# Layer 0 of a four-layer graph network: expert weights ordered behind adj's last rows, degree work ordered behind the expert blocks' outputs, and the last group's gate put in front of the blocks

## The chip, the cores and the metric

The kernel runs on one core of a Trainium2 chip. The core has TensorE (PE, matmuls, with its weight loads shown apart as PEld), VectorE (DVE), ScalarE (ACT), GpSimd (POOL) and SyncE (SP), which here only issues transfers. Each engine takes its instructions in the order in which the program holds them; semaphores tie the engines together. The metric is the device time of one execution in microseconds (us), lower is better.

## The reference, cut to what matters

There are N = 2708 nodes with 256 features each, a 2708 x 2708 matrix `adj`, and four layers, each a graph step followed by a feed-forward step. All numbers are float32. Only layer 0, and the row sums that layer 1 needs, are touched here:

```
x = x + weights(adj) @ (layernorm(x) @ W + B)         # weights = exp(-(1/r - 1)^2 / 0.5) where r < 1, else 0
h = layernorm(x)
top2 of (h @ Wg + bg) over 8 experts, softmax of the two
x = x + sum over the two of w * (gelu(h @ W1[e] + b1[e]) @ W2[e] + b2[e])
# layer 1, graph step
D = 1 / sqrt(sum of a row of (adj + I));  x = x + relu((D adj+I D) @ (layernorm(x) @ W) + b)
```

An expert has 256 x 1024 and 1024 x 256 weights. Layers 1 to 3 follow with other graph and feed-forward steps and are the same before and after.

## The kernel before, in words

The 2708 nodes are 22 tiles (`NT`) of 128 rows, the last with 20. The kernel is written against a tile framework: the Python code states the instructions, a scheduler chooses each engine's order by its own estimates, and semaphores are put in from the data dependences. `tc.add_manual_dep(..., NoSync, ...)` adds an order that the scheduler has to keep and no semaphore by itself. A pool's tile name with `bufs=n` has n buffers in turn; when a pool is closed its memory serves later pools, and what is first written there waits for the last use before.

**Adjacency of layer 0.** The target nodes are taken in three groups of 9, 7 and 6 tiles (`GROUPS`). For each group the loop over `j` (L712 and on) loads one row tile of `adjT` (`adrow`, L715, five buffers), ScalarE and VectorE turn it into weights (`weigh`, L699 to L704: Ln, Exp, a product, Exp, a mask), and PE multiplies it with `msg` into accumulators `acc` (L726). At the end of a group VectorE adds `acc` to `x` (L748).

**Gate of layer 0.** `send(tiles)` (L640 and on) runs after each group: layer norm statistics (`stats`), the normalised rows `xr` (L182 by `norm_to`), a turn by PE and a copy by ScalarE (`turn_to`, L195 and L196), the product with the 8 gate columns (L656) and the bias (`lg`, L658). Then come the two best experts (`top2_weights`), the place of each row in its expert's list (`route`, with matmuls at L344 and L346), and GpSimd's indirect scatters of the rows into `taken` in DRAM (L451). `xr` has one buffer, so the next group's `xr` waits until those scatters are done. After the second group, `blocks` makes the list of nine full blocks of 256 rows (`full`), and after the third the list of the rest (`rest`).

**Expert blocks of layer 0.** A block is 256 rows of one expert. `Blocks.run` (L523 and on) goes through 24 blocks (9 full, 15 of the rest). `fetch` (L490) reads the block's expert number into SyncE registers and issues the weight transfers `wa` (L620, W1 and its bias) and `wb` (L622, W2 and its bias), three sets of buffers in turn; `fetch_rows` gathers the rows `xs` (L465). PE turns the rows (`turn`, L518) and VectorE copies them into `xTs` (L520). PE multiplies with W1 (L547), ScalarE applies Gelu into `hTs` (L549), PE multiplies with W2 into `yacc` (L556), VectorE adds the bias and the gate's weight into `ys` (L558, L559), and GpSimd scatters `ys` into `given` (L451). The weights of blocks 0 and 1 and their rows are fetched inside the adjacency loop of the third group, at `j == NT - 5`.

**Degrees for layer 1.** Beside the blocks, `beside(b)` reads adj once more in 42 half rows of 677 KB (`adhalf`, L780, three buffers) and VectorE adds them up in `cs` (first copy L782, additions L784). It is called ahead of block b's matmuls, for row tile `j = b - 1`. After the blocks 22 small matmuls (L791) turn `cs` into the degrees.

Of the kernel before, what the change touches and what calls it, by code (L numbers as in the profile page):

```python
# [8 lines left out]
F32 = mybir.dt.float32  # L9
# [3 lines left out]
ALU = mybir.AluOpType  # L13
AX = mybir.AxisListType

P = 128
N = 2708
D = 256
# [18 lines left out]
def rows(t):  # L37
    return min(P, N - t * P)
# [28 lines left out]
def adj_ffn4(ctx: ExitStack, tc: tile.TileContext, a: dict, out: bass.AP):  # L67
# [122 lines left out]

    def turn_to(xT, xn, r):

        p = ps_tmp()
        for c in range(DC):
            te.transpose(p[:, c * P : c * P + r], xn[:, c * P : (c + 1) * P], ident[:r, :r])  # L195
        s.copy(xT, p[:, : DC * P].rearrange("p (c t) -> p c t", c=DC)[:, :, :r])  # L196
# [278 lines left out]
    class Blocks:  # L475
# [36 lines left out]

        def turn(self, pool, xs):
            xT = pool.tile([P, DC, 2 * P], F32, name="xTs", bufs=2)
            p = pools["psum"].tile([P, W], F32, name="turned", bufs=1)
            for k in range(2):
                for c in range(DC):
                    te.transpose(p[:, (c * 2 + k) * P : (c * 2 + k + 1) * P],  # L518
                                 xs[:, k, c * P : (c + 1) * P], ident)
            v.tensor_copy(xT.rearrange("p c t -> p (c t)"), p)  # L520
            return xT

        def run(self, pool, items, during=None):  # L523

# [88 lines left out]
    with ExitStack() as l0:  # L613
        hw = l0.enter_context(tc.tile_pool(name="h0", side="right", reuse_waits="tile", bufs=1))

        def weights0(b, es):

            pool, bufs = (hw, 2) if b % 3 < 2 else (hcs[0], 1)
            wa = pool.tile([P, 2048 + 8], F32, name="wa", bufs=bufs)
            nc.sync.dma_start(wa, a["L0_ffn_W1b"][bass.ds(es[0], 1)].rearrange("e p n -> p (e n)"))  # L620
            wb = pool.tile([P, 2048 + D], F32, name="wb", bufs=bufs)
            nc.sync.dma_start(wb, a["L0_ffn_W2p"][bass.ds(es[0], 1)].rearrange("e p n -> p (e n)"))  # L622
# [3 lines left out]
        hcs = []  # L626
        gate, gnn, sums = ExitStack(), ExitStack(), ExitStack()
# [12 lines left out]
        def send(tiles):  # L640

            G = len(tiles)
            t0 = tiles[0]
            st = stats(tiles)
            xr = tp.tile([P, GMAX, 2, XW], F32, name="xr", bufs=1)[:, :G]
            lg = tp.tile([P, G, E], F32, name="lg", tag=f"lg{G}", bufs=1)
            v.memset(lg[:, G - 1, :], 0.0)
            for i, t in enumerate(tiles):
                r = rows(t)
                norm_to(xr[:r, i, 0, :D], t, i, st)  # L650
                g.tensor_copy(xr[:r, i, 1, :D], xr[:r, i, 0, :D])
                xT = tp.tile([P, DC, P], F32, name="xT", bufs=2)
                turn_to(xT[:, :, :r], xr[:r, i, 0, :D], r)
                p = ps_tmp()
                for c in range(DC):
                    te.matmul(p[:r, :E], lhsT=xT[:, c, :r], rhs=wg[:, c, :],  # L656
                              start=(c == 0), stop=(c == DC - 1))
                v.tensor_tensor(lg[:r, i, :], p[:r, :E], bg[:r], ALU.add)  # L658
# [47 lines left out]
        for tiles in GROUPS:  # L706
# [5 lines left out]
            for j in range(NT):  # L712
                r = rows(j)
                ad = gp.tile([P, GMAX * P], F32, name="adrow", bufs=5)[:r, :w]
                nc.sync.dma_start(ad, a["adjT"][j * P : j * P + r, c0 : c0 + w])  # L715
                if tiles is GROUPS[0] and j % 2 == 0:
# [49 lines left out]
        cs = hp.tile([P, N], F32, name="cs")  # L766
        left = []

        def beside(b):

            j = b - 1
            if b == NA + 3:
                left.append(blocks_left(rest[2], MOST))
            if not 0 <= j < NT:
                return
            r = rows(j)
            for c0 in (0, N // 2):
                w = N // 2
                ad = hp.tile([P, N // 2], F32, name="adhalf", bufs=3)[:r]
                nc.sync.dma_start(ad, a["adjT"][j * P : j * P + r, c0 : c0 + w])  # L780
                if j == 0:
                    v.tensor_copy(cs[:, c0 : c0 + w], ad)  # L782
                else:
                    v.tensor_tensor(cs[:r, c0 : c0 + w], cs[:r, c0 : c0 + w], ad, ALU.add)  # L784

        work0.run(hc, items, beside)
        work0.run_rest(hc, more, left[0], ALWAYS)
# [760 lines left out]
```

The softmax here doesn't subtract the row's maximum and nothing guards it: scores larger than these inputs give would overflow.

## Time and profile before

| what | value |
|---|---|
| device time, median of 3 | 2094.61 us (2092.79 to 2096.02) |
| span of the profiled execution | 2097.1 us |
| PE busy | 1980.9 us, 94% of the span |
| DVE, ACT, POOL busy | 1100.6, 660.6, 288.1 us |
| mean granted clock of PE | 0.965 of full speed |
| read and written in DRAM | 206.46 MB, 20.65 MB |

In the trace the adjacency of layer 0 runs until about 272.7 us, the 24 blocks from there until 652.7 us, and layer 1 begins at about 664 us. All matmuls with 256 columns take two passes, so one matmul of the code is two in the trace: a block has 32 + 32 of them and 4 transposes.

How to read the lines shown below. A line of the timeline has the start in us from the span's start, the duration in us, the engine (SPq is SyncE's queue of transfers, for which the duration is that of issuing), the line of the code, the operation, the tile written and the tiles read, and how many instructions are merged. In brackets is the engine's idle time just before, and what ended it. A line of a table of windows has the window, its length, the busy time and count of PE, PEld, DVE, ACT and POOL, the clock granted to PE as a share of full speed, the busy share of the 16 DMA engines, and GB/s.

### The profile page before, as it was taken

The page shows a single profiled execution, that of the slowest core. Times are in us where ns is not written, and L with a number is a line of the kernel's source. Part 1 is how long each engine was busy: PE and PEld are TensorE (multiplying, and loading weights), DVE is VectorE, ACT ScalarE, POOL GpSimd, SP SyncE. Part 2 cuts the span into 40 slices and gives each one's busy share as a digit, 9 for nine tenths or more (in the row PEclk, how much of TensorE's full clock was granted, in tenths as well). Part 3 has the DMA queues.
Part 4 walks back from the last instruction along what each step waited for, and adds up shares of the span by engine and source line. Part 5 has one row for each costly group of instructions (what it writes and reads, how often), then busy time and mean ns, then how long its engine had stood idle before and what let it go on. Part 6 is the DMA issues. An engine that isn't in the chain of part 4 may idle for free.

```text
span 2097.1 us, 25890 instructions
## 1 busy us (share of the span) xinstructions
PE 1980.9 (94%) x9673; PEld 1424.7 (68%) x9673; DVE 1100.6 (52%) x2524; ACT 660.6 (31%) x1445; POOL 288.1 (14%) x315
## 2 busy tenths in 40 slices
PE   6999978999997999999899969999899999999997
PEld 5888767878885788878688848888566622232334
DVE  7677754544114323243331165455355488887876
ACT  7778732222222403022322351223243410120112
POOL 1004353333221000102142110000000000000000
PEclk9999989999997999999999989999899999999999
DMA  8435649987532442423265420000101000000000
GB/s 261 141 106 150 213 158 353 352 298 262 186 145 92 123 142 61 141 62 111 92 213 184 162 91 6 1 1 1 41 1 31 16 1 21 21 26 11 16 11 24
DMA packets 80611, 226.64 MB, mean 108 GB/s; under 512 B 15218, under 2 KB 38746, under 8 KB 71264
## 3 DMA queue, kind: packets, MB, share of 16 engines
q1 hardware_dynamic: 69056, 196.17, 28.4%
q0 software_dynamic: 11424, 28.74, 3.9%
q8 instruction: 80, 1.31, 0.3%
q14 instruction: 51, 0.42, 0.1%
HBM read 206.46 MB, written 20.65 MB: 108 GB/s over the span
## 4 chain that ended last, share of the span: by engine, by line
PE 57%; DMA 5%; issue 3%; DVE 2%; ACT 1%; POOL 1%; POOLq 0%; SPq 0%; DVEq 0%; ACTq 0%
PE num L1460 11%; PE ps_acc L1136 10%; PE acc L942 9%; PE ps_tmp L317 7%; PE den L1471 6%; DMA given<-ys,xs 4%; PE ps_acc L1312 3%; PE ps_tmp L238 3%; PE ps_acc L547 1%; PE ps_tmp L195 1%; PE ps_acc L238 1%; PE yacc L556 1%; PE ps_tmp L874 1%; DMA mine<-given 0%; POOL given L451 0%
## 5 line engine op out<-in xcount | busy, mean ns | idle before, releaser
L1455 DVE SCALAR_TENSOR_TENSOR e<-arena,G,mask 128x1024 f32<-128x1024 f32 (+2 forms) x264 | 294.1, 1149 | 44.0 <-PE den L1471 43.6
L556 PE MATMUL yacc<-wb,hTs 128*128 128x256 f32 x1152 | 267.5, 385 | 11.2 <-DVE ys L558 10.7
L556 PEld LDWEIGHTS yacc<-wb,hTs 128*128 128x128 f32 x1152 | 218.0, 193 | 44.0 <-DVE ys L558 14.6
L1460 PE MATMUL num<-e,wh 128*64 128x512 f32 (+4 forms) x1056 | 243.6, 558 | 0.0
L726 PE MATMUL acc<-msg,wt 128*128 128x256 f32 (+1 forms) x924 | 210.7, 386 | 7.9 <-DVE wt L704 7.9
L942 PE MATMUL acc<-sup,adrow 128*128 128x256 f32 (+1 forms) x924 | 214.4, 390 | 0.0
L1136 PE MATMUL ps_acc<-hh,e 128*128 128x257 f32 (+1 forms) x924 | 211.2, 386 | 0.0
L726 PEld LDWEIGHTS acc<-msg,wt 128*128 128x128 f32 (+1 forms) x924 | 175.7, 193 | 35.9 <-DVE wt L704 8.3
L942 PEld LDWEIGHTS acc<-sup,adrow 128*128 128x128 f32 (+1 forms) x924 | 176.6, 195 | 30.6 <-issue 5.5
L1136 PEld LDWEIGHTS ps_acc<-hh,e 128*128 128x128 f32 (+1 forms) x924 | 173.8, 193 | 29.6 <-issue 2.5
L547 PE MATMUL ps_acc<-xTs,wa 128*128 128x256 f32 x768 | 179.6, 385 | 8.7 <-DVE xTs L520 8.6
L1460 PEld LDWEIGHTS num<-e,wh 128*64 128x64 f32 (+1 forms) x1056 | 74.3, 138 | 155.2 <-issue 120.8
L549 ACT ACTIVATE hTs<-ps_acc,wa 128x256 f32<-128x256 f32 x192 | 89.9, 473 | 271.5 <-PE yacc L556 194.4
L547 PEld LDWEIGHTS ps_acc<-xTs,wa 128*128 128x128 f32 x768 | 142.1, 192 | 36.4 <-DVE xTs L520 11.4
L196 ACT COPY xT<-ps_tmp 128x256 f32<-128x256 f32 x126 | 43.0, 362 | 325.1 <-PE ps_tmp L195 324.0
L1471 PE MATMUL den<-e,wh 128*32 128x512 f32 (+4 forms) x1056 | 137.9, 551 | 0.0
L1133 DVE SCALAR_TENSOR_TENSOR e<-Rb,G,mask 128x640 f32<-128x640 f32 (+2 forms) x110 | 85.2, 775 | 97.1 <-PE ps_acc L1136 96.9
L451 POOL DMA_INDIRECT taken<-xr,r_ix x66 | 76.8, 1163 | 357.9 <-DVE b_vec L387 190.7
L451 POOL DMA_INDIRECT given<-ys,xs x72 | 81.8, 1136 | 229.9 <-DVE ys L559 166.0
L465 POOL DMA_INDIRECT xs<-taken,b_ix x72 | 87.2, 1212 | 189.0 <-DVE xTs L520 87.2
L919 DVE TENSOR_SCALAR mask<-adrow 128x1024 uint8<-128x1024 f32 (+1 forms) x66 | 41.6, 631 | 134.5 <-DMA adrow<-in_adjT 132.6
L558 DVE TENSOR_TENSOR ys<-yacc,wb 128x256 f32<-128x256 f32 x72 | 30.3, 421 | 155.2 <-PE yacc L556 155.0
(388 smaller groups left out, 2459.7 us busy)
## 6 DMA issues: line engine op xcount, KB each, us to landing
adhalf<-in_adjT SPq DMA_DIRECT2D x42, 677.0 KB
wb<-in_L_ffn_W2p SPq DMA_DIRECT2D x24, 1152.0 KB
wb<-in_L_ffn_Wdp SPq DMA_DIRECT2D x24, 1152.0 KB
wa<-in_L_ffn_W1b SPq DMA_DIRECT2D x24, 1028.0 KB
adrow<-in_adjT SPq DMA_DIRECT2D x42, 512.0 KB
adrow<-in_adjT SPq DMA_DIRECT2D x42, 320.0 KB
adrow<-in_adjT SPq DMA_DIRECT2D x21, 576.0 KB
adrow<-in_adjT SPq DMA_DIRECT2D x21, 448.0 KB
```

The costliest lines, as they stand in the source:

```text
L317: te.matmul(p[:, :w], lhsT=w1[:, c, f * P : (f + 1) * P], rhs=xnT[:, c, c0 : c0 + w], start=(c == 0), stop=(c == DC - 1))
L451: i = g.indirect_dma_start(out=dst, out_offset=bass.IndirectOffsetOnAxis(ap=ix, axis=0), in_=src, in_offset=None, bounds_check=bound, oob_ ...
L465: i = g.indirect_dma_start(out=dst, out_offset=None, in_=src, in_offset=bass.IndirectOffsetOnAxis(ap=ix, axis=0), bounds_check=bound, oob_ ...
L547: te.matmul(p[:, f % 2, :], lhsT=w1[:, c, f * P : (f + 1) * P], rhs=xT[:, c, :], start=(c == 0), stop=(c == DC - 1))
L549: s.activation(hT[:, f, :], p[:, f % 2, :], AF.Gelu, bias=bias[:, f : f + 1])
L556: te.matmul(q[:, k, :], lhsT=hT[:, f, k * P : (k + 1) * P], rhs=w2[k][:, f, :], start=(f == 0), stop=(f == HC - 1))
L726: te.matmul(p[:q, n - pair[0], :], lhsT=wt[:, k : k + q], rhs=msg[:r, j, :], start=(j == 0 and n == pair[0]), stop=(j == NT - 1 and n == p ...
L942: te.matmul(p[:q, n - pair[0], :], lhsT=ad[:, k : k + q], rhs=sup[:r, j, :], start=(j == 0 and n == pair[0]), stop=(j == NT - 1 and n == p ...
L1136: te.matmul(p[:q, : D + 1], lhsT=e[:r, k : k + q], rhs=hh[:r, j, :], start=(j == 0), stop=(j == NT - 1))
L1455: v.scalar_tensor_tensor(e[:r, :w], Rb[:r, k, :w], G[:r, j, 2 * pair + k, :], mask[:r, j, c0 : c0 + w], op0=ALU.max, op1=ALU.mult)
L1460: te.matmul(num[k * DK : (k + 1) * DK, hf, :q], lhsT=wh[:r, j, 2 * pair + k, :DK], rhs=e[:r, h0 - c0 : h0 - c0 + q], start=(j == 0), stop= ...
L1471: te.matmul(den[z : z + Q, :q], lhsT=wh[:ri, i, 2 * pair + k, DK : DK + 1].to_broadcast([ri, Q]), rhs=e[:ri, h0 - c0 : h0 - c0 + q], start ...
```

## The change: three orders in layer 0

1. **Expert weights behind adj's last rows.** `reads` collects adj's row loads, and each `wa` load is ordered behind the latest of them. The call of `work0.fetch` moves out of the loop over `j`, behind it, while `fetch_rows` stays. So the weight transfers no longer stand ahead of the rows that PE still needs.
2. **The last group's gate in front of the blocks.** The first turn of block 0's rows is ordered after the gate matmul of the last group's fourth tile (`gated[-3]`: the list has one entry for each tile of 22, and the third from its end is tile 19). The last group's statistics are split into the first two tiles and the other four, with the inverse root by Ln and Exp on ScalarE (`by_log`) instead of by twelve small VectorE operations, and its turns use the three `ps_acc` banks, which are free by then, instead of the two of `ps_tmp`.
3. **Degree reads and additions behind the blocks' outputs.** `beside` no longer reads from block 1 on. It starts at block 3, with three halves for each of blocks 3 to 8 and two for each of blocks 9 to 20, and adds a half one call after its read. Both the reads and the additions are ordered behind the latest scatter of a block's output (`given0`), so that VectorE does not stand at an addition while `ys` and `xTs` are behind it.

The amount of data and of arithmetic is the same but for these few operations.

```diff
-    def turn_to(xT, xn, r):
+    def turn_to(xT, xn, r, bank=None):
-        p = ps_tmp()
+        p = ps_tmp() if bank is None else bank
...
-        def turn(self, pool, xs):
+        def turn(self, pool, xs, after=None):
...
-                    te.transpose(p[:, (c * 2 + k) * P : (c * 2 + k + 1) * P],
-                                 xs[:, k, c * P : (c + 1) * P], ident)
+                    i = te.transpose(p[:, (c * 2 + k) * P : (c * 2 + k + 1) * P],
+                                     xs[:, k, c * P : (c + 1) * P], ident)
+                    if after is not None:
+                        tc.add_manual_dep(i.ins, after, mybir.DependencyInfo(
+                            mybir.DependencyClass.NoSync, mybir.DependencyReason.DATA),
+                            reason="order")
...
-            turned = self.turn(pool, self.rows[0])
+            turned = self.turn(pool, self.rows[0], after)
...
-            nc.sync.dma_start(wa, a["L0_ffn_W1b"][bass.ds(es[0], 1)].rearrange("e p n -> p (e n)"))
+            i = nc.sync.dma_start(wa, a["L0_ffn_W1b"][bass.ds(es[0], 1)].rearrange("e p n -> p (e n)"))
+            tc.add_manual_dep(i.ins, reads[-1], mybir.DependencyInfo(
+                mybir.DependencyClass.NoSync, mybir.DependencyReason.DATA), reason="order")
...
-            st = stats(tiles)
+            parts = [tiles]
+            if tiles is GROUPS[-1]:
+                parts = [tiles[:2], tiles[2:]]
+            st = {t: (z, t - part[0]) for part in parts
+                  for z in [stats(part, by_log=len(parts) > 1)] for t in part}
...
-                turn_to(xT[:, :, :r], xr[:r, i, 0, :D], r)
+                turn_to(xT[:, :, :r], xr[:r, i, 0, :D], r, ps_acc() if len(parts) > 1 else None)
...
+                gated.append(made.ins.name)
...
-                nc.sync.dma_start(ad, a["adjT"][j * P : j * P + r, c0 : c0 + w])
+                i = nc.sync.dma_start(ad, a["adjT"][j * P : j * P + r, c0 : c0 + w])
+                reads.append(i.ins.name)
...
                     for item in items[:2]:
-                        work0.fetch(item)
                         work0.fetch_rows(item)
+            for item in items[:2] if end else ():
+                work0.fetch(item)
...
+        halves = [(j, c0) for j in range(NT) for c0 in (0, N // 2)]
+        def behind_outputs(i):
+            tc.add_manual_dep(i.ins, scattered["given0"][-1].name, mybir.DependencyInfo(
+                mybir.DependencyClass.NoSync, mybir.DependencyReason.DATA), reason="order")
         def beside(b):
-            j = b - 1
...
-            if not 0 <= j < NT:
+            while read:
+                j, c0, ad = read.pop(0)
+                r, sums = rows(j), cs[:, c0 : c0 + N // 2]
+                behind_outputs(v.tensor_copy(sums, ad) if j == 0 else
+                               v.tensor_tensor(sums[:r], sums[:r], ad[:r], ALU.add))
+            if b < 3:
                 return
-            r = rows(j)
-            for c0 in (0, N // 2):
...
-        work0.run(hc, items, beside)
+            while halves and len(read) < (3 if b < NA else 2):
+                j, c0 = halves.pop(0)
+                ad = hp.tile([P, N // 2], F32, name="adhalf", bufs=3)
+                behind_outputs(nc.sync.dma_start(
+                    ad[: rows(j)], a["adjT"][j * P : j * P + rows(j), c0 : c0 + N // 2]))
+                read.append((j, c0, ad))
+        work0.run(hc, items, beside, gated[-3])
+        assert not halves and not read
```

More of the change, by code (lines that the diff above doesn't have):

```diff
@@ L517, in turn, with run @@
                 for c in range(DC):
-                    te.transpose(p[:, (c * 2 + k) * P : (c * 2 + k + 1) * P],
-                                 xs[:, k, c * P : (c + 1) * P], ident)
+                    i = te.transpose(p[:, (c * 2 + k) * P : (c * 2 + k + 1) * P],
[4 more added lines that the diff above has]
+                            reason="order")
             v.tensor_copy(xT.rearrange("p c t -> p (c t)"), p)
             return xT
-        def run(self, pool, items, during=None):
+        def run(self, pool, items, during=None, after=None):
             HC = 1024 // P
@@ L624, in weights0 @@
             return wa[:, :2048].rearrange("p (c h) -> p c h", c=DC), wa[:, 2048:], (w2, w2)
-        hcs = []
+        hcs, reads, gated = [], [], []
         gate, gnn, sums = ExitStack(), ExitStack(), ExitStack()
@@ L649, in send @@
                 r = rows(t)
-                norm_to(xr[:r, i, 0, :D], t, i, st)
+                norm_to(xr[:r, i, 0, :D], t, st[t][1], st[t][0])
                 g.tensor_copy(xr[:r, i, 1, :D], xr[:r, i, 0, :D])
                 xT = tp.tile([P, DC, P], F32, name="xT", bufs=2)
-                turn_to(xT[:, :, :r], xr[:r, i, 0, :D], r)
+                turn_to(xT[:, :, :r], xr[:r, i, 0, :D], r, ps_acc() if len(parts) > 1 else None)
                 p = ps_tmp()
                 for c in range(DC):
-                    te.matmul(p[:r, :E], lhsT=xT[:, c, :r], rhs=wg[:, c, :],
-                              start=(c == 0), stop=(c == DC - 1))
+                    made = te.matmul(p[:r, :E], lhsT=xT[:, c, :r], rhs=wg[:, c, :],
+                                   start=(c == 0), stop=(c == DC - 1))
+                gated.append(made.ins.name)
                 v.tensor_tensor(lg[:r, i, :], p[:r, :E], bg[:r], ALU.add)
@@ L766, in adj_ffn4 @@
         cs = hp.tile([P, N], F32, name="cs")
-        left = []
+        left, read = [], []
+        halves = [(j, c0) for j in range(NT) for c0 in (0, N // 2)]
+        def behind_outputs(i):
+            tc.add_manual_dep(i.ins, scattered["given0"][-1].name, mybir.DependencyInfo(
+                mybir.DependencyClass.NoSync, mybir.DependencyReason.DATA), reason="order")
         def beside(b):
-            j = b - 1
             if b == NA + 3:
                 left.append(blocks_left(rest[2], MOST))
-            if not 0 <= j < NT:
-                return
-            r = rows(j)
-            for c0 in (0, N // 2):
[L778 to L784, printed above, removed]
-        work0.run(hc, items, beside)
+            while read:
[4 more added lines that the diff above has]
+            if b < 3:
+                return
+            while halves and len(read) < (3 if b < NA else 2):
[6 more added lines that the diff above has]
+        assert not halves and not read
         work0.run_rest(hc, more, left[0], ALWAYS)
```

## The prediction

> **What bounds the kernel now.** I read the page's busy line first (PE 94% of the span), so a gain can only be PE idle time or PE time at a low clock. The edits lie in layer 0 alone: both instruction orders agree from layer 1 on. So I took a table of windows over 200 to 740 us, looked for stretches where PE is not busy, and opened the timeline there. The queue of transfers comes first:
>
> ```profile
> 243.72 0.35 SPq L620 DMA_DIRECT2D wa<-in_L_ffn_W1b  x1
> 244.25 0.34 SPq L622 DMA_DIRECT2D wb<-in_L_ffn_W2p  x1
> 245.10 0.33 SPq L620 DMA_DIRECT2D wa<-in_L_ffn_W1b  x1
> 245.62 0.65 SPq L622 DMA_DIRECT2D wb<-in_L_ffn_W2p  x1
> 246.37 1.06 SPq L715 DMA_DIRECT2D adrow<-in_adjT  x2
> ```
>
> Two experts' weights (2 x 2180 KB) go out before the last two rows of adj. The timeline shows who pays:
>
> ```profile
> 261.53 0.83 ACT L141 ACTIVATE y<-adrow,tiny 128x640 f32<-128x640 f32 x1 [9.73 <-DMA adrow<-in_adjT]
> 266.25 6.46 PE L726 MATMUL acc<-msg,wt 128*128 128x256 f32 x20 [7.91 <-DVE wt L704]
> 266.28 0.20 POOL L660 COPY xr<-choice 128x12 int32<-128x12 int32 x1 [3.85 <-DMA taken<-xr,r_ix]
> ...
> 318.76 0.87 DVE L782 COPY cs<-adhalf 128x1354 f32<-128x1354 f32 x1 [12.82 <-DMA adhalf<-in_adjT]
> ...
> 320.02 5.82 PE L556 MATMUL yacc<-wb,hTs 128*128 128x256 f32 x16 [8.67 <-DVE ys L558]
> ```
>
> PE stands 7.91 us for adj's last rows, and 8.67 us because VectorE, which works in order, stands 12.82 us at the first degree copy with the output ys behind it. The POOL line matters later: xr is only free at 266.28, when the scatters of the middle group have landed. A third stall of the second kind:
>
> ```profile
> 425.22 0.49 DVE L507 MEMSET xs<- 128x516 f32 x1 [8.31 <-DMA given<-ys,xs]
> ...
> 427.78 2.08 PE L547 MATMUL ps_acc<-xTs,wa 128*128 128x256 f32 x4 [3.24 <-DVE xTs L520]
> ```
>
> The windows give the clock after it, and the two regimes of the blocks:
>
> ```profile
> 427.50:430.00 2.50, 2.22 (x5) 1.85 (x6) 2.30 (x4) 0.00 (x0) 2.19 (x2) 0.50 0.77 228
> ...
> 340.00:425.00 85.00, 82.78 (x389) 69.69 (x387) 42.45 (x50) 22.33 (x48) 31.23 (x21) 1.00 0.94 354
> ...
> 515.00:620.00 105.00, 105.00 (x504) 90.74 (x503) 18.91 (x42) 27.80 (x59) 26.54 (x26) 1.00 0.51 181
> ```
>
> While adj is read again for the degrees (340 to 425), DMA is 94% busy at 354 GB/s; once the reads are over, PE never idles. There a block takes 14.27 us (weights issued at 531.37 and 545.64). That is the floor: 64 matmuls at 0.2155 us (83.8 us of warm PE time over 389 of them, 340 to 425) and four transposes.
>
> **What the Trainium skill says.** "TensorE: Matmul & The Clock Gate", What's actually happening: an idle window of about 3.4 us halves PE's clock, and about 3.4 us of sustained work restores it. The trace agrees: 0.50 after the 3.24 us gap, and 16 matmuls in 5.82 us after the 8.67 us one, 3.62 us elsewhere. So removing a long stall also returns 2 to 3 us of slow matmuls. "DMA: Bandwidth & Descriptors", Issuing engines are not separate DMA queues: transfers of SyncE and GpSimd interleave on the same 16 engines. The trace agrees: given scatters hold the memset for 8.31 us while adhalf and weights stream.
>
> **The change, part by part.**
>
> *Weights behind adj's last rows.* In the new order both rows precede the four weight transfers. The rows (370 KB) then need about 1 us at 354 GB/s and can't be what ScalarE waits for at 251.8. From there its chain for two rows, 5.6 us measured from 261.53 to the last wt at 267.15, ends near 257.5, before PE is through its earlier rows (258.34). So PE goes straight on: 20 matmuls x 0.22 = 4.4, end at 262.7 instead of 272.7. The weights go out about 3 us later and land (4.46 MB at 390 GB/s, the rate of 255 to 265) near 260, still ahead of use.
>
> *Gate in front.* The ten us can't all reach the blocks. The gate's first norm writes xr, so it waits for the POOL copy: 266.5. The rest of its start fits: sums and two tiles' statistics 2.8 us from 262.7, then Ln and Exp on 128x2. The trace has no such activation; the nearest, 128x6, takes 0.21, a floor is the 0.17 of small VectorE operations; I take 0.21 each. They replace twelve small VectorE operations (2.4 us). Six tiles at 1.48 us (spacing of the lg additions at 282.32 and 283.80, with blocks' matmuls between), somewhat faster here from three banks: 6 us, then the copy xTs, 0.7. The first expert matmul starts near 274, now 276.13. The gathers of its rows are issued at 267.07 and 268.46 as now and are in by 272.65 at the latest. Taking the turn after the third-last tile's gate costs nothing more.
>
> What follows on PE: 12 matmuls cold, 0.39 each as now (12 in 4.72): 278.7. The route's 14 matmuls, 1.9: 280.6. Then the second xTs copy stands behind 14 small VectorE operations (3.4 us) and takes 0.7; PE waits for it: 285. After that nothing is missing: 46 matmuls of block 0, 64 of block 1, 4 of block 2, 24.6 us, two turns within: 310. The same point is now at 325.68, after 8.67 us of stall, the cold stretch behind it, and the gate between blocks. **Gain 15.7.** ScalarE's three table loads (1.28 each, same number) fall into the waits. GpSimd's 12 scatters now stand ahead of both outputs of block 0; ys has two buffers and block 2 rewrites the first at about 318, long after 301 (12 x 1.27 from 286), so that wait is covered.
>
> *Degree reads and additions.* 42 reads of 677 KB stay, three a block from block 3, two from block 9, each added a block later behind the outputs. Now from 325.68 to the last yacc at 652.7 is 327.0 us; 22 blocks at the floor less the four matmuls, plus a microsecond of degree matmuls, is 314.1. The excess is 12.9, of which 6.3 is the one interval with the stall at 425 (421.19 to 441.79). After: three additions (3 x 1.52) start when ys is out and end about 6 us into a block, when VectorE has nothing else due; xTs is wanted at 14. A block with three reads moves 2.23 MB weights, 2.08 reads, 0.53 gathers and scatters: 4.84 MB, 13.7 us at 354 GB/s, under 14.27 but barely; with two, 4.15 MB, 11.7. The memset behind the given scatter stays on VectorE ahead of xTs, so some waits stay: I keep 4 us between bounds 0 and 12.9. **Gain 8.9.**
>
> The added waits order engines only; queued behind them are ys and xTs, which the floor of 515 to 620 shows have slack. The reads end with block 20 and the additions with 21 of 23, so the degree matmuls don't move. Memsets and the split of the stats go beside PE work.
>
> Sum 24.6: 2094.6 - 24.6 = 2070.
>
> **The rivals.**
> *Smaller gain.* The start stays bound by gathers, cold clock and the route, DMA near 95% still holds VectorE: 8 at the start, 2 later, 2085. For it: the 13.7 of 14.27 us, and xr free only at 266.28. Against: the saturated stretch shrinks from some 13 blocks to 6.
> *Everything goes.* Degree excess zero (12.9), VectorE's wait after the route filled (3) and the blocks two us earlier: 33.6, so 2061. For it: 515 to 620 without a gap. Against: the xr release.
> *Slower.* VectorE's small operations and table loads are exposed with PE cold, leaving 2 of the 15.7; and reads wait for additions, additions for reads without overlap: 4.6 + 5.9 + 6.3 (2.23 MB weights) = 16.8 a block, 15 us over six blocks, 4 won in the others: 2104. For it: three buffers, three reads. Against: each addition frees its own buffer at once.
> *Nothing.* The two losses cancel: 2094.
>
> **How the numbers follow.** Forecast 0.64 (2062 to 2079), smaller gain 0.18, everything 0.09, nothing 0.03, slower 0.06. Leaving out slower, nothing, and the outer parts of the two gain cases gives 2060 to 2085. Faster 0.91, same 0.03, slower 0.06.
>
> **What would show it.** Right: no ACT wait for adrow near 252, the adjacency's last matmul near 263; first expert matmul at 273 to 275; a PE gap of 2 to 5 us around the route; no gap near 310; last yacc near 628 (652.7 - 24.6). Wrong: an expert matmul waiting for wa or wb, a start after 278, or VectorE waiting for adhalf with ys or xTs behind it in blocks 4 to 9, seen as PE gaps and clock 0.5.

## The result and the profile after

The changed kernel takes 2078.04 us (median of 4 runs, 2076.05 to 2081.6), the kernel before 2093.73 in the same comparison: ratio 0.9925, 95% interval 0.9908 to 0.9943, so 15.7 us less. The forecast was 2070, range 2060 to 2085. A second measurement of the unchanged code of the changed kernel, made later among the experiments, gave 2069.75; why the two differ is half of what follows.

Spans differ by some us from one execution to the next before layer 0's adjacency is over, so times are best compared from a common instruction. I take **A**, the start of PE's last uninterrupted stretch of adjacency matmuls, just behind the small matmul of L261: 238.65 before, 237.29 after. The first lines to look at are of the timeline of the changed kernel:

```profile
237.29 24.20 PE L739 MATMUL acc<-msg,wt 128*128 128x256 f32 x110
...
247.21 0.83 ACT L141 ACTIVATE y<-adrow,tiny 128x640 f32<-128x640 f32 x1 [0.36 <-DMA adrow<-in_adjT]
...
260.24 0.69 DVE L762 TENSOR_TENSOR x<-x,acc 128x512 f32<-128x512 f32 x1 [4.95 <-PE acc L739]
...
267.50 0.21 POOL L672 COPY xr<-choice 128x12 int32<-128x12 int32 x1 [5.94 <-DMA taken<-xr,r_ix]
267.60 0.41 DVE L182 TENSOR_SCALAR xr<-x,mv,var 128x256 f32<-128x256 f32 x1 [3.32 <-DMA taken<-xr,r_ix]
...
268.07 1.12 PE L195 MATMUL ps_acc<-ident,xr 128*128 128x128 f32 x4 [6.57 <-DVE xr L182]
...
279.10 4.33 PE L551 MATMUL ps_acc<-xTs,wa 128*128 128x256 f32 x12 [2.12 <-DVE lg L670]
```

ScalarE's wait for adj's row has shrunk from 9.73 us to 0.36, and PE goes through 110 adjacency matmuls without a gap. The sum into x starts at A + 22.95, before at A + 32.81. Then everything waits for one thing: at 267.50 the scatters of the middle group have landed, GpSimd and VectorE may write xr again, and PE, idle for 6.57 us, begins the gate. The gate needs 11 us, so the first expert matmul is at 279.10.

One thing that now lies beside these scatters shows in the queue of transfers of the changed kernel:

```profile
261.52 0.33 SPq L629 DMA_DIRECT2D wb<-in_L_ffn_W2p  x1
```

This is block 2's W2, 1152 KB. It goes out as the last matmul of the adjacency ends, in the kernel before at 272.75, 6.5 us after the copy at 266.28 that shows xr free. The adjacency now ends some 10 us earlier, and this transfer goes out while the last of the scatters is being issued (260.58 to 261.56).

The second place is block 1. PE and then ScalarE in the timeline of the changed kernel (a releaser "issue" is idle time for which the profile shows no cause, "remote" one that it can't place):

```profile
298.42 4.50 PE L551 MATMUL ps_acc<-xTs,wa 128*128 128x256 f32 x20
306.98 4.21 PE L551 MATMUL ps_acc<-xTs,wa 128*128 128x256 f32 x8 [4.06 <-issue]
310.98 4.54 PE L560 MATMUL yacc<-wb,hTs 128*128 128x256 f32 x16
```

```profile
302.93 0.47 ACT L553 ACTIVATE hTs<-ps_acc,wa 128x256 f32<-128x256 f32 x1 [2.09 <-PE ps_acc L551]
306.45 0.47 ACT L553 ACTIVATE hTs<-ps_acc,wa 128x256 f32<-128x256 f32 x1 [3.04 <-issue]
308.59 0.97 ACT L553 ACTIVATE hTs<-ps_acc,wa 128x256 f32<-128x256 f32 x2 [1.67 <-remote]
```

Both engines stand still in the middle of a block whose weights and rows are there, and the 8 matmuls that follow take 4.21 us where four take 1.03 warm. PE goes on at 306.98, just as the Gelu of 306.45 ends (306.92), so its part looks like a wait for ScalarE to empty an accumulator; what holds ScalarE, the profile doesn't say. I call this **the stop**.

Third, the blocks with the degree reads, in a table of windows of the changed kernel (columns as before):

```profile
340.00:425.00 85.00, 85.00 (x406) 73.33 (x405) 39.98 (x52) 22.26 (x47) 30.53 (x24) 1.00 0.87 337
427.50:430.00 2.50, 2.50 (x13) 2.21 (x12) 1.24 (x3) 0.00 (x0) 0.84 (x1) 1.00 1.04 428
515.00:620.00 105.00, 104.97 (x499) 89.94 (x498) 39.59 (x57) 26.51 (x56) 32.87 (x25) 1.00 0.59 222
```

PE is busy in every one of the 85 us in which 82.78 were busy before, at full clock, with DMA at 0.87 instead of 0.94. The degree work itself now looks like this in the timeline of VectorE:

```profile
349.15 1.64 DVE L797 COPY cs<-adhalf 128x1354 f32<-128x1354 f32 x2
350.70 1.56 DVE L798 TENSOR_TENSOR cs<-cs,adhalf 128x1354 f32<-128x1354 f32 x1
```

No wait stands in brackets: the halves have been there since the block before. The memset of xs still waits for scatters of given (42.2 us in total, 51.8 before), but at most 4.9 us at a time (8.3 before), which the slack of the block covers. Another 20.0 us ahead of it, at most 5.2 at a time, have no releaser in the profile. From block 1's last matmul to the last yacc it is 315.3 us, against 327.0 before and a floor of 314.1.

### The profile page after: what moved, and what is told of

Its sections match the earlier page's. It is cut to its first block, busy times and chain, and to the rows that moved or that the text cites. A ratio compares the mean times of both kernels' runs of the same rounds, so it can differ in the third digit from the quotient of the medians.

```text
span 2075.3 us, 25886 instructions
## 1 busy us (share of the span) xinstructions
PE 1974.2 (95%) x9673; PEld 1422.3 (69%) x9673; DVE 1098.1 (53%) x2513; ACT 661.8 (32%) x1449; POOL 287.4 (14%) x315
## 3 DMA queue, kind: packets, MB, share of 16 engines
q8 instruction: 80, 1.31, 0.3%
## 4 chain that ended last, share of the span: by engine, by line
PE 55%; DMA 5%; issue 3%; DVE 2%; ACT 2%; POOL 1%; POOLq 0%; DVEq 0%; SPq 0%; ACTq 0%
PE num L1483 11%; PE acc L965 9%; PE ps_acc L1159 9%; PE ps_tmp L317 7%; PE den L1494 6%; DMA given<-ys,xs 4%; PE ps_acc L1335 3%; PE ps_tmp L238 3%; PE ps_tmp L195 1%; PE ps_acc L238 1%; PE ps_tmp L897 1%; POOL xs L465 1%; PE ps_acc L551 1%; POOL given L451 0%; DMA mine<-given 0%
## 5 line engine op out<-in xcount | busy, mean ns | idle before, releaser
L560 PE MATMUL yacc<-wb,hTs 128*128 128x256 f32 x1152 | 263.1, 381 | 0.9 <-DVE ys L562 0.7
L451 POOL DMA_INDIRECT given<-ys,xs x72 | 91.8, 1275 | 208.7 <-DVE ys L563 161.2
L942 DVE TENSOR_SCALAR mask<-adrow 128x1024 uint8<-128x1024 f32 (+1 forms) x66 | 41.5, 629 | 134.4 <-DMA adrow<-in_adjT 134.2
L465 POOL DMA_INDIRECT xs<-taken,b_ix x72 | 75.0, 1042 | 191.0 <-DVE xTs L524 90.6
```

Source lines behind the costliest of these rows:

```text
L451: i = g.indirect_dma_start(out=dst, out_offset=bass.IndirectOffsetOnAxis(ap=ix, axis=0), in_=src, in_offset=None, bounds_check=bound, oob_ ...
L465: i = g.indirect_dma_start(out=dst, out_offset=None, in_=src, in_offset=bass.IndirectOffsetOnAxis(ap=ix, axis=0), bounds_check=bound, oob_ ...
L560: te.matmul(q[:, k, :], lhsT=hT[:, f, k * P : (k + 1) * P], rhs=w2[k][:, f, :], start=(f == 0), stop=(f == HC - 1))
```

## The experiments

Three sets, each on one chip and each set on a different one, with runs of the kernel before among them (medians 2093.51, 2095.1 and 2093.81). In the table "block 1 done" is the point that the prediction called blocks 0 and 1 done and four matmuls of block 2; times are us from A in each kernel's profiled run. The forecast row is the prediction's own points, less before's A.

| kernel | first expert matmul | block 1 done | end of last yacc | median, us | ratio to before |
|---|---|---|---|---|---|
| before | 37.5 | 87.0 | 414.0 | 2093.73 | |
| forecast | 35.4 | 71.4 | 389.4 | 2070 | |
| changed | 41.8 | 82.4 | 397.7 | 2078.04 | 0.9925 [0.9908, 0.9943] |
| *first set* | | | | | |
| part 1 undone | 47.4 | 88.6 | 404.5 | 2084.63 | 0.9947 [0.9927, 0.9967] |
| part 2 undone | 36.5 | 84.1 | 399.5 | 2080.29 | 0.9934 [0.9917, 0.9952] |
| part 3 undone | 41.2 | 87.5 | 412.9 | 2087.29 | 0.9975 [0.996, 0.999] |
| twenty copies | 41.5 | 80.5 | 395.7 | 2075.51 | 0.9911 [0.9894, 0.9927] |
| *second set* | | | | | |
| own tile for the last rows | 37.4 | 72.7 | 388.2 | 2070.54 | 0.9871 [0.9849, 0.9892] |
| scatters late | 40.2 | 73.4 | 388.1 | 2072.53 | 0.9886 [0.9866, 0.9907] |
| W2 of block 3 late | 40.0 | 74.0 | 389.6 | 2072.15 | 0.9881 [0.9861, 0.9902] |
| own tile, scatters late | 37.3 | 72.5 | 388.6 | 2071.17 | 0.988 [0.9855, 0.9905] |
| *third set* | | | | | |
| changed, again | 40.0 | 74.4 | 390.1 | 2069.75 | 0.9893 [0.9878, 0.9908] |
| two more reads | 40.2 | 74.6 | 390.0 | 2071.37 | 0.9892 [0.9878, 0.9906] |
| own tile, W2 late | 37.4 | 72.5 | 387.7 | 2067.68 | 0.9885 [0.9869, 0.99] |
| own tile, gate between | 36.2 | 74.1 | 389.8 | 2071.93 | 0.989 [0.9871, 0.991] |

Behind the last yacc the code is the same in all of them, and the profiled runs spend between 1431 and 1444 us there. So a difference of a few us between medians says little about layer 0 by itself; the times from A say more, but each is from one run.

### Part 1 undone

```diff
                     for item in items[:2]:
+                        work0.fetch(item)
                         work0.fetch_rows(item)
-            for item in items[:2] if end else ():
-                work0.fetch(item)
```

(and the order of `wa` behind `reads[-1]` taken out).

> The changed kernel with its first part undone: the weights of blocks 0 and 1 are issued ahead of adj's last two rows again. If those rows set the end of the adjacency and with it the start of the gate, PE idles some 8 us at the last rows again, the last adjacency matmul ends near 272 instead of 260, and the gate's first norm moves from 267.6 to about 275: 8 to 10 us more, 2086 to 2088. If the start is held by the scatters and gathers whatever the adjacency does, PE idles but nothing behind it moves: 2078 to 2080.

The waits of the adjacency are back, in the timeline of this kernel:

```profile
264.95 0.83 ACT L141 ACTIVATE y<-adrow,tiny 128x640 f32<-128x640 f32 x1 [9.44 <-DMA adrow<-in_adjT]
...
269.67 6.39 PE L736 MATMUL acc<-msg,wt 128*128 128x256 f32 x20 [7.62 <-DVE wt L713]
```

The sum into x starts at A + 32.44 again, and the end of the last yacc is 6.8 us later than the changed kernel's by the profile, 6.6 by the medians (the intervals of the two ratios just overlap). It is less than the 9.5 us that the adjacency loses, and a second time says why: GpSimd's copy that shows xr free comes at A + 27.7 here and at A + 27.6 in the kernel before, but at A + 30.2 in the changed one. So part 1 itself pushes the release of xr back by 2.5 us. Two things that it does can account for this: the weights of blocks 0 and 1 go out later, and block 2's W2 goes out with the earlier end of the adjacency (here at 276.09, 6.0 us after that copy). At the 415 GB/s that the engines move then, the 1152 KB of W2 take 2.8 us (an estimate). No run separates the two. (In the kernels with an added tile W2 goes out at A + 19.7, and the copy still comes at A + 29.7 to 30.0; there too it lies beside the scatters.)

### Part 2 undone

```diff
-            if tiles is GROUPS[-1]:
-                parts = [tiles[:2], tiles[2:]]
...
-        work0.run(hc, items, beside, gated[-3])
+        work0.run(hc, items, beside)
```

> The changed kernel with its second part undone: the last group's gate is free to go between the matmuls of the first blocks, its statistics are in one piece and by VectorE. If the gate in front earns its place, the blocks lose again what the gate takes between them (7 to 8 us of PE time and the route's waits): 2083 to 2087. If standing in front costs as much as it brings (in the changed kernel PE is at half clock and mostly idle from 265 to 279, first expert matmul 279.1, three us later than before the change), the first expert matmul moves to 272 to 274 and the time is 2072 to 2079.

The expert matmuls begin 5.4 us earlier (A + 36.5), as soon as the gathered rows are in, in PE's timeline:

```profile
273.01 0.69 PE L518 MATMUL turned<-ident,xs 128*128 128x128 f32 x2 [9.48 <-DMA xs<-taken,b_ix]
...
275.79 5.24 PE L551 MATMUL ps_acc<-xTs,wa 128*128 128x256 f32 x12 [0.78 <-DVE xTs L524]
```

The gate then stands between the matmuls of block 0, and the lead is gone when 68 expert matmuls are done: A + 61.4 here, A + 61.1 in the changed kernel. The further lag, 1.7 us by the end of block 1, comes in the stop, which holds VectorE too here: `yacc` is complete at 311.85, but its sum into ys starts at 317.72 (9.27 us idle, releaser "remote"), and PE waits for it:

```profile
318.20 5.38 PE L560 MATMUL yacc<-wb,hTs 128*128 128x256 f32 x16 [5.49 <-DVE ys L562]
```

The medians differ by 2.3 us and the intervals overlap: the gate in front costs about what it brings.

### Part 3 undone

`beside` as in the kernel before (one row tile a block from block 1, nothing ordered behind the outputs).

> The changed kernel with its third part undone: degree reads and additions from block 1 on, as before. If the trace's account holds (12.9 us of excess over the block floor before, 1.2 after), it loses 11.7 us at least, and the 8.7 us stall at the first degree copy with its cold clock may return on top: 2089 to 2099, with clock 0.5 after a PE gap. If the third part is worth only the 4 to 9 us that the prediction gave it: 2082 to 2087.

Windows of this kernel, to be held against 85.00 of 85.00 above:

```profile
335.00:380.00 45.00, 43.96 (x209) 37.43 (x207) 22.29 (x25) 11.26 (x24) 16.42 (x12) 1.00 0.94 358
380.00:425.00 45.00, 43.16 (x196) 36.46 (x197) 24.20 (x29) 11.12 (x24) 19.19 (x12) 0.96 0.91 337
425.00:520.00 95.00, 91.14 (x423) 77.30 (x423) 41.72 (x56) 22.36 (x48) 36.82 (x26) 0.98 0.75 279
```

PE loses 6.7 us in these three windows alone, and block 1's end to the last yacc takes 325.4 us, nearly before's 327.0. By the medians part 3 is worth 9.3 us, the largest of the three. By the profile it is 15.2 (412.9 against 397.7), but the profiled run, 2092.67, is among the slowest of 13 (2084.13 to 2093.96). The three losses (6.6, 2.3 and 9.3, each against the changed kernel of the first pair, which was not in this set) add up to 18.2, a little more than the 15.7 of the whole, which at this spread is no contradiction.

### Twenty copies: is the stop tied to a place in ScalarE's program?

```diff
+            for n in range(20 if end else 0):
+                pad = small.tile([P, 1], F32, name="pad")
+                i = s.copy(pad, ones)      # ordered behind the last weights' Exp
             send(tiles)
```

> The changed kernel with 20 one-column ScalarE copies put behind the last adjacency weights, where ScalarE waits some 8 us for the sums. In both traces ScalarE stops at its 269th instruction or so, counted in the program's order (before at 305.5 for 3.8 us, after from 300.8 to 306.5), with nothing in the trace that it waits for, just behind a packet of the instruction queue (304 and 298). If it is ScalarE's instruction supply, the stop moves 20 instructions earlier in the work, off block 1: no PE gap of 4 us near 303, no half clock behind it, about 7 us less, 2070 to 2073. If it waits for data of block 1 or for crowded transfers, the stop stays at the same Gelu of block 1 and the time at 2077 to 2081.

The stop is still in block 1, 20 instructions further on in ScalarE's program, spread over more Gelus. PE's timeline of this kernel:

```profile
308.42 1.13 PE L552 MATMUL ps_acc<-xTs,wa 128*128 128x256 f32 x4 [1.75 <-ACT hTs L554]
310.56 2.07 PE L552 MATMUL ps_acc<-xTs,wa 128*128 128x256 f32 x4 [1.01 <-issue]
```

That speaks against a fixed place in ScalarE's stream. It is shorter, and the time 2.5 us lower than the changed kernel's, which no theory had asked for.

### Own tile for the last group's rows

```diff
-                norm_to(xr[:r, i, 0, :D], t, st[t][1], st[t][0])
-                g.tensor_copy(xr[:r, i, 1, :D], xr[:r, i, 0, :D])
+                xn = xr[:r, i, 0, :D] if own is None else own[:r, i, :]
+                norm_to(xn, t, st[t][1], st[t][0])
+                if own is not None:
+                    g.tensor_copy(xr[:r, i, 0, :D], xn)
+                g.tensor_copy(xr[:r, i, 1, :D], xn)
```

> The last group's normalised rows go into a tile of their own (xn_end); two GpSimd copies a tile bring them into xr, so VectorE and PE no longer wait for the middle group's scatters to leave xr. If it is the release of xr that starts the gate late, its first turn comes near 264.5 instead of 268.1; the gate still takes some 11.5 us with PE cold, so the first expert matmul comes near 275.5 instead of 279.1, and the time falls by 3 to 4 us. If block 0's rows (in at about 272.5), the cold clock or the table loads set the start of the blocks, the first expert matmul stays after 278 and the time falls by less than 1.5 us. The stop in block 1 (306.98 in the changed kernel) is expected in both cases, and if it is tied to a fixed moment of the transfers rather than to block 1, the start's gain is lost there again.

In this kernel's timeline PE's wait ahead of the gate falls to 3.14 us, and the gate is under way when GpSimd's copy comes, at 270.31, A + 29.7, about where it comes in the other kernels (the profile names PE as what released it here):

```profile
267.92 1.12 PE L195 MATMUL ps_acc<-ident,xn_end 128*128 128x128 f32 x4 [3.14 <-DVE xn_end L182]
...
270.31 0.20 POOL L678 COPY xr<-choice 128x12 int32<-128x12 int32 x1 [5.77 <-PE ps_tmp L673]
```

From A the gate starts 3.0 us earlier than in the repeated changed kernel (27.3 against 30.3), the first expert matmul is 2.7 earlier, and block 1 ends 1.6 earlier: the release of xr did hold the gate. The rest of the gain goes at the second xTs copy behind the route, for which PE waits 1.31 us here and 0.39 there. In the time it can't be told from nothing (2070.54 against 2069.75, in different sets).

### Scatters late, and W2 of block 3 late

```diff
-                for k in range(2):
-                    scatter(taken[0], ix[:r, i, k : k + 1], xr[:r, i, k, :], 2 * N - 1, "taken0")
...
+            if b == 2:
+                later.pop()()              # the same 12 scatters, ordered behind given0's latest
+                past.extend(scattered["taken0"])
+                gate.close()
```

```diff
-            nc.sync.dma_start(wb, a["L0_ffn_W2p"][bass.ds(es[0], 1)].rearrange("e p n -> p (e n)"))
+            i = nc.sync.dma_start(wb, a["L0_ffn_W2p"][bass.ds(es[0], 1)].rearrange("e p n -> p (e n)"))
+            if b == 3:
+                behind(i, scattered["given0"][1:2])
```

> The twelve scatters of the last group's rows are issued behind block 1's outputs instead of ahead of block 0's; every engine but GpSimd keeps its order, and nothing needs these rows before the gathers for block 9. If the stop of ACT and PE in block 1 (4.06 us, and some 7.7 us with the cold matmuls after it) comes from those scatters and block 3's W2 sharing the transfer engines, it leaves block 1: no gap over 1 us there, the twenty-second W1 and W2 stretch warm, point 'four matmuls of block 2' at about 312 instead of 319.7, and the time falls by 5 to 8 us unless a stop of the same kind comes where the scatters now are (316 to 332), which would give it back. If the stop has nothing to do with the scatters (a supply of instructions at a fixed place, or the W2 transfer alone), it stays at 303 to 309 and the time stays within 1.5 us.

> The W2 transfer of block 3 (1152 KB, issued at 299.07) waits until block 0's second output has landed (about 308); no instruction moves. If the stop in block 1 needs this transfer beside the twelve scatters, it goes or shrinks to under 1.5 us, and the time falls by 4 to 7 us. If the scatters alone make it, or neither does, it stays and the time is the same within 1.5 us.

> Both edits together: own tile for the last group's normalised rows and the scatters behind block 1's outputs. If both waits are what holds the start, the gains add: first expert matmul near 275.5, no stop in block 1, blocks 0 and 1 and four matmuls of block 2 done near 308 to 310 (the forecast's 310), 9 to 12 us faster than the changed kernel, about 2067. If the start is bound elsewhere, no more than the better of the two edits alone.

The stop is in none of the three: block 1 is done at A + 73.4, 74.0 and 72.5 instead of 82.4. Read alone, each looked like a proof of its theory. But it was gone from the own-tile kernel of the same set too, where the scatters and the W2 transfer lie over block 1 as in the changed one. So neither edit was shown to remove anything, and the unedited kernel had to be run again.

### The changed kernel again

> The changed kernel once more, nothing edited. Four kernels whose edits don't all touch the last group's scatters or block 3's W2 transfer showed no stop of ACT and PE in block 1. If the stop belongs to the changed kernel's own order and timing, it is there again: a PE gap of about 4 us near 303 to 307, clock 0.5 after it, and a time near 2078, 5 to 8 us above the kernels without it. If it comes and goes from one execution or one chip to the next, the profile may be free of it, last yacc ends near 628 to 630, and the time is near 2071 to 2074.

ScalarE's and PE's timeline of that run, at the place of the stop:

```profile
299.94 6.22 PE L551 MATMUL ps_acc<-xTs,wa 128*128 128x256 f32 x28
...
302.75 0.47 ACT L553 ACTIVATE hTs<-ps_acc,wa 128x256 f32<-128x256 f32 x1 [0.39 <-PE ps_acc L551]
303.62 0.47 ACT L553 ACTIVATE hTs<-ps_acc,wa 128x256 f32<-128x256 f32 x1 [0.39 <-PE ps_acc L551]
...
306.00 3.62 PE L560 MATMUL yacc<-wb,hTs 128*128 128x256 f32 x16
```

Same code, no stop: a Gelu every 0.86 us, PE without a gap, and block 1 done at A + 74.4 instead of 82.4. The 8.0 us between the two are nearly all of the 8.3 us between 2078.04 and 2069.75. When block 1's long run of matmuls begins (298.42 and 299.94) the two kernels are 0.6 us apart from A; the other 7.4 us are the stop and the cold matmuls after it. The transfer engines were as full as in the run with the stop: 0.89 busy at 261 GB/s from A + 61.6 to A + 68.1, against 0.87 at 253 there, with the same scatters going on. So full engines and scatters don't suffice to make it.

All six profiles of the first pair and of the first set show ScalarE slowed or held in block 1, that of before included:

```profile
309.26 0.47 ACT L549 ACTIVATE hTs<-ps_acc,wa 128x256 f32<-128x256 f32 x1 [3.75 <-remote]
```

None of the eight profiles of the second and third set does. So the stop goes with the chip or the occasion of a set, not with this change; which of the two was not tested. The kernel before takes the same time in all sets (2093.5 to 2095.1), and its profile offers the reason: behind the held Gelu PE waits 8.67 us for ys in any case, and that wait ends when VectorE has got adj's half at 318.76, not when the Gelu is done. The changed kernel has no such wait, so the stop shows in its time. With part 2 undone, where no degree copy is in the way, VectorE was held until A + 78.4, in the kernel before until A + 80.9, which fits. Still, this last step is argued: before was not profiled in a set without the stop.

### Two more reads, meant to crowd block 1

```diff
+            if b == 1:
+                extra = hc.tile([P, N // 2], F32, name="extra", bufs=1)
+                for c0 in (0, N // 2):
+                    nc.sync.dma_start(extra, a["adjT"][:P, c0 : c0 + N // 2])
```

> Two more reads of 677 KB (half rows of adj, into a tile that nothing uses) behind block 3's W2 transfer, so that the transfer engines stay full from about 299 to 307 beside the last scatters; no engine but the queue of transfers has another instruction. If full transfer engines in block 1 make the stop, it is there, longer than 4 us, ending after 309, and the time rises by 2 to 6 us over the changed kernel of the same call. If transfers have no part in it, the stop is as in the unedited kernel of this call, and the time is the same within 1.5 us.

This one missed. The two reads were issued at 260.7 and 274.5, long before block 1; they crowded nothing there. The time (2071.37) and the profile are the changed kernel's, so all that it shows is that 1.39 MB more in that stretch cost no measurable time.

### Own tile, with W2 late, and with the gate between

The first joins the two edits shown above. The second keeps the own tile and undoes part 2 as shown.

> The two cheapest edits together: own tile for the last group's normalised rows, and block 3's W2 behind block 0's second output. If the own tile gives the gate its earlier start (first turn about 3 us after the adjacency's last matmul instead of 6) and no stop follows, the last yacc ends near 627 to 629 and the time is 2068 to 2071. If the gain at the gate is lost at the second xTs copy behind the route, as the 1.31 us wait there hinted, it is as fast as either edit alone, 2070 to 2072.

> Part 2 of the change undone (no order of block 0's turn behind the gate, statistics in one part on VectorE, two banks for the turns), with the own tile for the last group's rows kept, so that neither the gate nor the turn waits for the scatters' release of xr. If the gate in front of the blocks is worth its place, this is 2 to 4 us slower than the own tile with the gate in front (2070.5). If it costs about what it brings, as undoing it alone hinted (2 us, inside the spread), the two are within 1.5 us of each other.

Own tile and late W2 give the lowest median of all, 2067.68, and the earliest end by the profile (A + 387.7, 2.4 us ahead of the repeated changed kernel). It beats both kernels in median; from the changed kernel of the same set the intervals don't separate it, and by the ratio to before the own tile alone stands lower (0.9871 against 0.9885). With the gate between the blocks' matmuls, PE starts on the experts only when the gathers are in (277.32, after 9.24 us of waiting for them) and block 1 ends 1.7 us later than with own tile, W2 late and the gate in front. So the gate in front is worth a microsecond or two once xr is out of its way. By medians that is 2071.93 against 2070.54 for the own tile alone, and 2067.68 with W2 late: the direction agrees, the intervals overlap. As the changed kernel has it, with xr in its way, the gate in front brings nothing that shows: block 1 ends at A + 74.4 there and at A + 74.1 with the gate between.

## Why the prediction was right, and where it was not

The forecast and the first measurement differ by 8 us, the forecast and the second by a quarter of a microsecond. Neither is by itself a verdict on the steps:

- **Weights behind adj's last rows: right.** Forecast 10 us off the adjacency's end; measured from A, 32.81 - 22.95 = 9.9. What it left out is that transfers then lie beside the middle group's scatters, whose landing moves from A + 27.6 to A + 30.2 (29.8 in the repeat). It had the weights of blocks 0 and 1 land near 260 and took the release of xr, 266.5, from the kernel before; it counted neither block 2's W1 (issued at 257.02) nor its W2 (261.52), and the engines stay full until about 268. The Trainium skill's "DMA: Bandwidth & Descriptors", Issuing engines are not separate DMA queues, says that transfers interleave on the same 16 engines whichever engine started them. The windows of the repeated changed kernel agree: the scatters' last 5.5 us, from 263.67 to 269.18, are spent with the engines full.

```profile
262.00:265.00 3.00, 1.62 (x8) 1.06 (x6) 2.61 (x7) 0.00 (x0) 1.36 (x2) 0.90 1.00 415
265.00:270.00 5.00, 0.26 (x1) 0.27 (x2) 2.13 (x11) 0.70 (x3) 0.24 (x2) 0.50 1.02 424
270.00:275.00 5.00, 4.81 (x22) 3.79 (x21) 2.12 (x10) 1.64 (x6) 4.08 (x4) 0.50 0.31 93
275.00:280.00 5.00, 4.22 (x21) 3.49 (x20) 1.74 (x9) 1.85 (x3) 3.79 (x4) 0.50 0.37 97
280.00:285.00 5.00, 5.00 (x15) 3.99 (x13) 2.06 (x11) 3.25 (x4) 4.39 (x9) 0.51 0.43 110
```

- **The gate starts at xr's release: right in kind, 2 to 2.5 us early.** Forecast 266.5, which is A + 27.9; measured A + 30.3 and A + 29.9. The own tile showed that it is this release that holds it: without it the gate starts at A + 27.3.
- **"Six tiles at 1.48 us", first expert matmul near 274: wrong.** From the first norm to the first expert matmul I gave 7.5 us; it takes 11.5 and 10.2. The failed term is the 6 us for the six tiles, cut from 6 x 1.48 = 8.9 for the three banks, which nothing had measured. In the repeat PE works through the tiles and block 0's four turns from 269.74 to 278.65, 8.9 us with 0.15 of idle time, so PE sets the pace and not the banks. It is cold: PE has just stood for 6 us, and the windows above show clock 0.50 from 265 until past 280. The gate matmuls of one tile take 0.93 us here and took 0.51 between warm expert matmuls. (The 11.5 of the first pair has 1.3 us more, at the last lg; what held that is not known.) The forecast's own warning sign, a start after 278, came true. PE's timeline of the repeat:

```profile
269.74 1.12 PE L195 MATMUL ps_acc<-ident,xr 128*128 128x128 f32 x4 [6.12 <-DVE xr L182]
...
273.89 0.93 PE L667 MATMUL ps_tmp<-L_ffn_Wg,xT 128*128 128x8 f32 x4
...
278.17 0.48 PE L518 MATMUL turned<-ident,xs 128*128 128x128 f32 x1
279.43 5.49 PE L551 MATMUL ps_acc<-xTs,wa 128*128 128x256 f32 x12 [0.78 <-DVE xTs L524]
```

- **The wait after the route: wrong the other way.** I had PE wait until 285 for the second xTs copy. It waits 0.38 us. From the route's last matmul to PE's going on I had 4.4 us (280.6 to 285); in the changed kernel it is 2.2 (284.89 to 287.11), most of it filled with other matmuls. The wrong term is the 3.4 us of small VectorE operations ahead of the copy: it is 1.4 (284.93 to 286.37). So the first expert matmul is 4.7 us later than forecast in the repeat (A + 40.0 against 35.4), and block 1's end only 3.0 us (74.4 against 71.4). Two terms of the sum were wrong and partly cancelled.
- **"After that nothing is missing": wrong in the first pair and the first set, right in the two later ones.** The stop is what was missing from the sum. Of the 15.7 us forecast for the start, 4.7 were measured there (87.0 - 82.4) and 12.7 in the repeat (87.0 - 74.4).
- **Degree work: right, and larger.** I kept 4 us of excess over the floor of 314.1; it is 1.2 us, and 1.6 in the repeat. The gain is 11.7 and 11.3 instead of 8.9. With three reads a block DMA stands at 0.87, not near the 0.95 of the smaller-gain rival, and the memset's longest wait for a scatter is 4.9 us instead of 8.3. (Two points of the working: there are 44 reads, the last two of 20 rows with block 21, which moves nothing; and the 83.8 us behind the pace of 0.2155 is not in the line shown, which has 82.78. The pace itself holds: in the changed kernel it is 3.45 us from the first of 16 yacc matmuls, at 326.17, to the next matmul, at 329.62.)

The sum to the last yacc was forecast as 24.6 us; it is 16.4 in the first pair and 24.0 in the repeat. The hit within a quarter of a microsecond is in part luck: the start brought 3.0 us too little and the degrees 2.4 too much. The first measurement, 2078.04, lies 8 us above the forecast for a reason that the forecast did not have, the stop. Of the rivals, the smaller gain named part of the right causes for the start (xr's late release, the cold clock), yet had the degrees at 2 us, where they turned out to be the largest part. Nothing spoke for the slower case: no addition waits for its read.

## What to carry to other kernels

A wait that is removed uncovers what lay under it: before, VectorE's wait at the degree copy covered a stop of several us that the change didn't bring, and as far as the one profile of before tells, only the changed kernel pays for it. When an edit makes an odd gap vanish, run the unedited kernel again beside it before believing the edit; three edits looked like cures here until the kernel without them was as fast. A transfer that starts when a stage ends moves with that end: ask what it will then lie beside, as block 2's W2 came to lie beside the scatters. And a duration read from a stage with warm PE is not the duration of the same work behind a wait: take the clock of the place it moves to.

## What the runs showed of the hardware

- The stop: 4.06 us in which PE waits for nothing that the profile names, over 0.06 us after a held Gelu of ScalarE ends; with twenty copies and with part 3 undone the profile does name ScalarE (waits of 1.75 and of 1.93 and 2.39 us). With part 2 undone VectorE is held as well (5.9 us past the end of `yacc`). It occurs in one set and not in others, for one code. It doesn't sit at a fixed instruction of ScalarE (twenty copies), and full transfer engines with scatters beside them don't suffice to make it (the repeat). What makes it was not found.
- "TensorE: Matmul & The Clock Gate", What's actually happening, gives about 3.4 us of sustained work until the clock is full. The gate's small matmuls didn't do it: PE is busy for 4.81 us of 270 to 275 and stays at 0.50. From the first expert matmul on it took about 3.0 us in the changed kernel (279.1 to 282.1) and 5.5 in the repeat (279.4 to 284.9).
- The prediction took the 3.24 us gap of the kernel before as agreeing with the idle window of about 3.4 us that it quotes. It is shorter, and a gap of 2.85 us with part 3 undone is shorter still and was enough: the clock was full until 321 and 0.50 from 322 to 325, and 16 matmuls took 5.41 us instead of 3.62. In PE's timeline of that kernel:

```profile
320.95 5.41 PE L560 MATMUL yacc<-wb,hTs 128*128 128x256 f32 x16 [2.85 <-DVE ys L562]
```

- Scatters: xr is shown free 5.5 to 6.0 us after GpSimd is done issuing the last scatter of the middle group, in the repeat while the engines move 415 to 424 GB/s in all; in the kernel before, where they run empty 2 us after that issue, it takes 3.9.
